# Shared expert's matmuls dealt out anew between the end of attention, the expert count, the token table and the first routed expert

## Chip, core and metric

One core of one Trainium2 chip. The metric is the device time of one launch in microseconds, lower is better. The kernel before took 885.71 us as the median of three runs (885.13 to 885.71). Its profiled execution took 885.71 us too, with a span from first to last instruction of 883.9 us.

## What is computed

Two layers in float32 on x of 16 x 128 tokens by 512. The first is cross attention with 32 query heads of 16 and 8 key heads, whose keys and values are both the context. The second is a mixture of 32 routed experts (hidden size 256) with 8 of 32 chosen per token, and one shared expert that every token passes:

```python
x = x + xattn(layernorm(x), ctx, ctx)
h = layernorm(x)
scores = sigmoid(h @ gate_weight.T)
# 4 of 8 groups by the sum of their two best, then the 8 best experts; weights * 2.5
routed = sum_e comb[:, e] * ((silu(h @ w1[e].T) * (h @ w3[e].T)) @ w2[e].T)
shared = (silu(h @ shared_w1.T) * (h @ shared_w3.T)) @ shared_w2.T
out = x + routed + shared
```

## The kernel before, in words

Line numbers are those of the kernel before. The order of instructions on PE, DVE, ACT and POOL is the order in which the program writes them (a manual schedule, line 199 on); each engine goes through its own list in order, and a matmul that waits holds back all matmuls behind it. Only waits between engines are added by the framework: for data, and for a buffer of a pool whose earlier user still reads it.

The work runs in stages:

1. *Attention* (`attention_small`), over 32 items (16 batches, two halves of the key heads): `scores`, `values`, `transposes`. While it ends, the second layernorm's rows are made (`gate_rows`), stored for the gathers, transposed into `xnT` (`turn_of`), and gate logits are taken (`gate_parts`, `gate_sums`). PSUM, eight banks of 128 x 512 float32, is shared by `ps_sc` (two tiles of two banks), `ps_x` (two banks), `ps_lg` and `ps_oT` (one each).
2. *Routing* (`route`): DVE works out the choice of experts; PE counts tokens per expert (lines 1230 and 1238), ranks them (1261 to 1280) and orders the experts (1274 to 1310).
3. *Token table*: for each of 16 token tiles, `slot_tokens` has DVE make two one-hot tiles `hr` and `hq` (line 1018), ACT scale one into `ht` (1029), and PE add eight products into `tok` (1033). `finish_tokens` (1044, 1045) turns `tok` into the table `token` that the gathers index.
4. *Routed experts*: POOL gathers token rows with indirect DMAs (1440) into eight buffers; DVE transposes them in blocks (1489); ACT and DVE copy the blocks into halves of `xall` (1486); PE multiplies. The first expert runs directly (`up`, 1521), the next 30 by a scheme of seven products (1592), for which DVE makes sums of weights (1554) and differences of tokens (1583). Expert outputs (1729) are scaled by ACT and added to the output by indirect DMAs (1701).

The *shared expert* has no stage of its own: its matmuls are fillers. `shared_up(k, i, ...)` is a generator of eight matmuls of 128x512 for token block k (of 4) and half i of the hidden size (of 2): four into a bank g (then ACT's silu, line 290), four into a bank u (then DVE's product, 293). `shared_down(b)` is two matmuls for token tile b (1370), and `add_down` adds them to x on DVE (1380) and stores x to the output. There are 64 up matmuls and 16 downs. Ups of (0,0) are drawn by `filler(n)` in attention, the other 56, in the order (0,1), (1,0), (1,1), (2,0), (2,1), (3,0), (3,1), by `up_matmuls(n)`:

| where drawn | up matmuls before |
|---|---|
| attention's end: `filler` 1, 1, 1, then 5 | 8 |
| `route`, ahead of the count (line 1138) | 20 |
| `route`, behind the ranks (1311, 1326) | 4 + 9 |
| token steps b = 0 to 6, one each (1402) | 7 |
| behind the table (1776, 1780), two calls of `2 * ND` | 8 + 8 |

Downs 0 to 7 stand at the odd token steps, downs 8 to 15 behind the last ups. There, each down is followed on DVE's list by a transpose of gathered rows, some copies, and the add of that down.

In this stretch PSUM holds `ps_y` and `ps_z` (one bank each, used in turn by the downs, and later by the routed experts' outputs), `ps_gu` (two banks for the ups), `ps_rt` (`tok` and the rank) and `ps_sm` (two small tiles). Silus and products are collected in the lists `later` and `products` and written by `evictions`, which holds a product back for one token step. Behind the last down, `ps_p` opens with six banks, in the place of `ps_gu`, `ps_rt` and `ps_sm`; the routed experts use it as a ring. The pool `late`, with the sums and the silu results of the routed experts, lies where x lay, so its first users wait for the stores of x.

Of the kernel before, what the change touches and what calls it, by code (L numbers as in the profile page):

```python
# [9 lines left out]
F32 = mybir.dt.float32  # L10
# [5 lines left out]
PSUM = bass.MemoryType.PSUM  # L16
DRAM = bass.MemoryType.DRAM

P = 128
# [27 lines left out]
def tile_xattn_moe(  # L47
# [22 lines left out]
    TB = 512  # L70
# [160 lines left out]
    def gate_rows(b, eng):  # L231
        xn = xnp.tile([P, D], F32, tag="xn2", name="xn2", bufs=4)
        normalized(xn, xs[b], b, SECOND, eng)
        nc.sync.dma_start(rows[ts(b, P), 0:D], xn)
        xn2[b] = xn
# [39 lines left out]
    def shared_up(k, i, bank, later, products):  # L275


        g, u = bank(), bank()
        sl = fp.tile([P, TB], F32, tag="ssl", name="ssl")
        for w, acc in ((0, g), (1, u)):  # L280
            for d in range(ND):
                nc.tensor.matmul(  # L282
                    acc,
                    lhsT=sup[:, w, d, ts(i, P)],
                    rhs=xnT[k][:, d, :],
                    start=(d == 0),
                    stop=(d == ND - 1),
                )
                if d == ND - 1 and w == 0:
                    later.append(lambda: nc.scalar.activation(sl, g, AF.Silu))  # L290
                if d == ND - 1 and w == 1:
                    products.append(
                        lambda: nc.vector.tensor_tensor(acts[k][:, i, :], sl, u, ALU.mult)
                    )
                yield
# [5 lines left out]
    def attention_small():  # L301


        with ExitStack() as ph:
# [134 lines left out]
            H = P // 2  # L439
            halves = [slice(h * H, (h + 1) * H) for h in range(2)]  # L440

            def transposes(*sets, pool=ps_x, between=()):


                x = pool.tile(
                    [P, 2, 2, 2, P], F32, tag=("x" if pool is ps_x else "sc"), name="x"
                )
                for s, (of, split, _) in enumerate(sets):
                    for k in range(4):
                        for h, rows in enumerate(halves):  # L450
                            if split:
                                to = x[:, h, :, s, ts(k, P // 4)]
                                by = ident[rows, rows].rearrange("p (a b) -> p a b", a=2)
                            else:
                                to = x[:, h, k // 2, s, ts(k % 2, H)]
                                by = ident[rows, rows]
                            nc.tensor.matmul(  # L457
                                to,
                                lhsT=of[rows, k, :],
                                rhs=by,  # L460
                                start=True,
                                stop=True,
                                is_transpose=True,
                                tile_position=(h * H, 0),
                            )
                for s, (_, _, then) in enumerate(sets):
                    if s == len(sets) - 1:
                        for f, a in between:
                            f(*a)
                    then(x[:, :, :, s])  # L470
# [29 lines left out]
            def values(b, i):  # L500
                oT = ps_oT.tile([P, TB], F32, tag="oT", name="oT")
                for j in range(NJ):
                    nc.tensor.matmul(  # L503
                        oT[j * HP : (j + 1) * HP],
                        lhsT=vas[b // 4 % 2][:, b % 4, 2 * j + i, :],
                        rhs=ps.pop((b, i, j)),
                        start=True,
                        stop=True,
                        tile_position=(0, j * HP),
                    )  # L510
                t = ap2.tile([P, G, P], F32, tag="oTs", name="oTs")
                nc.vector.tensor_copy(
                    t.rearrange("p g (h s) -> p h g s", h=2),
                    oT.rearrange("p (h g s) -> p h g s", h=2, g=G),
                )
                oTs[b, i] = t
# [15 lines left out]
            def added(b, i, eng=nc.gpsimd):  # L532
                return (
                    oTs.pop((b, i)),
                    True,
                    lambda x: add(b, i, x.rearrange("p h r (g e) -> p (h r) g e", e=HP), eng),
                )

            def turn_of(b, copy=nc.scalar.copy):
                def then(x):  # L540
                    copy(
                        xnT[b // 4][:, :, ts(b % 4, P)].rearrange(
                            "p (r k) (h s) -> p h r k s", r=2, h=2
                        ),
                        x.rearrange("p h r (k s) -> p h r k s", k=2),
                    )

                return xn2.pop(b).rearrange("p (k d) -> p k d", d=P), False, then
# [12 lines left out]
            def gate_parts(b):  # L561
                lgT = ps_lg.tile([P, 2 * P], F32, tag="lg", name="lgT")
                for k in range(ND):
                    nc.tensor.matmul(  # L564
                        lgT[k * E : (k + 1) * E],
                        lhsT=gw[:, k, :],
                        rhs=xnT[b // 4][:, k, ts(b % 4 // 2, 2 * P)],
                        start=True,
                        stop=True,
                        tile_position=(0, k * E),  # L570
                    )
                parts_of[b] = ap2.tile([P, 2 * P], F32, tag="lgTs", name="lgTs")
                nc.scalar.copy(parts_of[b], lgT)
# [106 lines left out]

            gate_rows(12, nc.gpsimd)
            nc.scalar.activation(table, table, AF.Sigmoid)
            values(*items[N - 1])
            transposes(added(*items[N - 2]), turn_of(11), pool=ps_sc)
            gate_rows(13, nc.gpsimd)
            gu = ps_sc.tile([P, 2, TB], F32, tag="sc", name="gu")
            banks = iter([gu[:, i] for i in range(2)])
            later, products = [], []
# [2 lines left out]
            def filler(n):  # L691
                for _ in range(n):
                    next(matmuls)

            transposes(added(*items[N - 1], nc.vector))
            gate_parts(8)
            layernorm_stats(14, SECOND)
# [6 lines left out]
            gate_sums(10, nc.scalar.copy)  # L704
            filler(1)
            transposes(turn_of(12), turn_of(13))
            gate_parts(12)
            gate_rows(15, nc.vector)
            transposes(turn_of(15), pool=ps_sc)
            gate_rows(14, nc.vector)  # L710
            transposes(turn_of(14, nc.vector.tensor_copy))
            gate_sums(12, nc.scalar.copy)
            gate_parts(14)
            gate_sums(14, nc.scalar.copy)
            filler(5)
            return later, products

    def attention_general():
# [328 lines left out]
    def experts(ups, in_order, later, products):  # L1047
# [64 lines left out]
                )  # L1112
            last[:] = [dma.ins]

        def bank():
            return ps_gu.tile([P, TB], F32, tag="gu", name="gu")

        def all_ups():
            for k, i in ups:
                yield from shared_up(k, i, bank, later, products)  # L1120

        matmuls = all_ups()
# [5 lines left out]
        def route():  # L1128
# [6 lines left out]

            sg = new([P, NT, E], "sg")
            nc.scalar.activation(sg, logits, AF.Sigmoid)
            up_matmuls(20)
            for silu in later:
                silu()  # L1140
            later.clear()
# [181 lines left out]
            nc.vector.tensor_copy(order, owner[0:1, :])  # L1323
            for k in range(NW):
                load_weights(k, True, True)
            up_matmuls(9)
            slots = new([P, NT, TOPK], "slots", home="hi")
            for b in range(NT):
                nc.vector.max(slots[:, b, :], key[:, b, :])
# [34 lines left out]

            return sr, sq, weights, flags

        def shared_down(b):
            y = (ps_y, ps_z)[b % 2].tile([P, D], F32, tag="y", name="y")
            for i in range(NI):
                nc.tensor.matmul(  # L1370
                    y,
                    lhsT=acts[b // 4][:, i, ts(b % 4, P)],
                    rhs=sdn[:, i, :],
                    start=(i == 0),
                    stop=(i == NI - 1),
                )
            products.append(lambda: add_down(b, y))
# [17 lines left out]
        for b in range(NT):  # L1395
            slot_tokens(b, sr, sq, tok, oh, evictions())
            if b == 2:
                weights()
            if b == 6:
                flags()  # L1400
            if b < 2 * ND - 1:
                up_matmuls(1)
            if b % 2:
                shared_down(next(downs))
        finish_tokens(token, tok, oh)
        early.close()
        tp = ctx.enter_context(tc.tile_pool(name="tp", bufs=2))
        pieces = []
        for k in range(E):
# [374 lines left out]
        n_copied = 3  # L1784
        downs = list(downs)
        for i, b in enumerate(downs):
            shared_down(b)
            transpose_to(min(6 + i, last_slice(3)))
            for f in copies[len(copies) * i // len(downs) : len(copies) * (i + 1) // len(downs)]:
                f()  # L1790
            for f in products:
                f()
            products.clear()
        shared.close()
        ps_p = ctx.enter_context(tc.tile_pool(name="ps_p", bufs=6, space=PSUM))
        x_only.close()
        late = ctx.enter_context(tc.tile_pool(name="late", bufs=2, side="right"))
        KEPT = 2
# [169 lines left out]
```

## Time and profile before

| what | value |
|---|---|
| profiled execution | 885.71 us |
| its span | 883.9 us |
| mean granted TensorE clock | 0.994 |
| chain that ended last, share of PE | 86% |
| of it: seven products (L1592), outputs (L1729), shared ups (L282), shared downs (L1370) | 42%, 24%, 5%, 2% |
| first to last attention matmul, about | 1 to 109 us |
| count begins / table done / first routed matmul | 141.60 / 186.53 / 219.73 us |

The profile is of one execution. A row of the timeline is: start in us, length in us, engine, line, operation, output<-inputs, shape, and in brackets the idle time of the engine ahead of it with what ended it. A float32 matmul of the program shows as two records, so 16 records of line 282 are one group's eight ups. Ends of matmuls are modelled, and a length reaches past the start of the next; starts are the better measure. Equal rows that follow each other are merged (x count). A row of waits is: who waited, for whom, total us, times, longest.

### The profile page before, as it was taken

Reading aid. Unit: us, or ns where it says so; the run is one execution under the profiler, and the core shown is the slowest. Engines: PE = TensorE matmul, PEld = TensorE weight load, DVE = VectorE, ACT = ScalarE, POOL = GpSimd, SP = SyncE. Lnnn points to the kernel's source line nnn. Section 1 sums busy time; section 2 is a strip of 40 time slices with the busy share of each in tenths; the row PEclk is TensorE's granted clock in tenths of the full one; section 3 lists DMA queues with packets and bytes.
Section 4 is the critical chain, followed back from the end, with each engine's and each line's share of the span. In section 5 each row is a group of like instructions: output and inputs, shape, how many; then the busy total and the mean of one; then the engine's idle time right before and its main releaser. Section 6 shows DMA issues by size and latency. Waiting matters only on the chain.

```text
span 883.9 us, 13625 instructions
## 1 busy us (share of the span) xinstructions
PE 864.2 (98%) x4015; PEld 540.4 (61%) x4015; DVE 626.0 (71%) x1599; ACT 689.6 (78%) x1570; POOL 479.3 (54%) x590
## 2 busy tenths in 40 slices
PE   9999989998999999999999999999999999999995
PEld 5344444543766665666666666666767777777763
DVE  7877767766887677777777777777768777777510
ACT  5888832437899898878888889898898989999831
POOL 4487550044255576656566655665555456664554
PEclk9999999999999999999999999999999999999998
DMA  9111112547367788777778777878778767776544
GB/s 303 60 48 49 49 49 86 181 150 210 109 163 163 167 195 202 165 175 185 174 172 190 182 181 187 184 191 201 196 154 196 179 165 172 197 191 163 92 76 55
DMA packets 59876, 137.15 MB, mean 155 GB/s; under 512 B 12168, under 2 KB 16392, under 8 KB 59792
## 3 DMA queue, kind: packets, MB, share of 16 engines
q0 software_dynamic: 32032, 69.25, 40.8%
q1 hardware_dynamic: 27680, 66.81, 22.3%
q8 instruction: 34, 0.56, 0.3%
q14 instruction: 50, 0.41, 0.2%
q10 hardware_dynamic: 80, 0.13, 0.0%
HBM read 96.71 MB, written 46.73 MB: 162 GB/s over the span
## 4 chain that ended last, share of the span: by engine, by line
PE 86%; issue 3%; DVE 3%; POOL 3%; DMA 2%; ACT 1%; another core or an unknown queue 0%; SPq 0%; POOLq 0%; DVEq 0%; ACTq 0%
PE p L1592 42%; PE y L1729 24%; PE gu L282 5%; PE sc L487 4%; PE oT L503 3%; POOL out_dram L1701 3%; PE y L1370 2%; PE x L457 2%; DMA out_dram<-yw,token 2%; PE gu L1521 2%; DMA cn<-in_c_dram 1%; DVE blocks L1489 1%; PE tok L1033 1%; PE lgT L564 0%; PE lg L579 0%
## 5 line engine op out<-in xcount | busy, mean ns | idle before, releaser
L1486 ACT COPY xall<-blocks 32x256 f32<-32x256 f32 (+10 forms) x1137 | 419.0, 369 | 15.1
L1701 POOL DMA_INDIRECT out_dram<-yw,token x150 | 245.1, 1634 | 211.0 <-DMA out_dram<-yw,token 73.9
L1729 PE MATMUL y<-wdn,sa 128*128 128x512 f32 (+2 forms) x672 | 259.1, 594 | 0.0
L1440 POOL DMA_INDIRECT xgs<-rows,token x138 | 154.5, 1119 | 137.1 <-DVE token L1045 57.2
L1592 PE MATMUL p<-xall,wup 128*128 128x270 f32 (+27 forms) x720 | 185.5, 394 | 0.0
L1592 PEld LDWEIGHTS p<-xall,wup 128*128 128x128 f32 x720 | 136.6, 190 | 44.3 <-issue 16.6
L1729 PEld LDWEIGHTS y<-wdn,sa 128*128 128x128 f32 (+2 forms) x672 | 100.9, 171 | 83.7 <-issue 71.7
L1745 ACT ACTIVATE yw<-y,wt 128x512 f32<-128x512 f32 x138 | 94.8, 687 | 70.7 <-PE y L1729 39.3
L1592 PE MATMUL p<-t,s 128*128 128x270 f32 (+27 forms) x480 | 125.6, 394 | 0.0
L1592 PEld LDWEIGHTS p<-t,s 128*128 128x128 f32 x480 | 91.1, 190 | 37.6 <-issue 22.4
L1489 DVE STREAM_TRANSPOSE blocks<-xgs 128x512 f32<-128x512 f32 x138 | 97.4, 706 | 0.2
L1602 DVE TENSOR_TENSOR z<-u,p 128x270 f32<-128x270 f32 (+27 forms) x96 | 48.8, 508 | 68.7 <-PE p L1592 64.5
L497 ACT ACTIVATE p<-sc 128x1024 f32<-128x1024 f32 x64 | 62.1, 1023 | 13.2 <-PE sc L487 13.2
L1592 PE MATMUL p<-t,wup 128*128 128x270 f32 (+27 forms) x240 | 63.8, 396 | 0.2 <-DVE z L1602 0.2
L1592 PE MATMUL p<-xall,s 128*128 128x270 f32 (+27 forms) x240 | 63.5, 395 | 0.4 <-DVE z L1602 0.4
L1592 PEld LDWEIGHTS p<-t,wup 128*128 128x128 f32 x240 | 44.9, 190 | 25.4 <-issue 14.8
L282 PE MATMUL gu<-xall,sup 128*128 128x512 f32 x128 | 58.1, 599 | 0.7 <-ACT ssl L290 0.7
L1602 DVE TENSOR_TENSOR u<-u,p 128x270 f32<-128x270 f32 (+27 forms) x48 | 24.4, 508 | 44.8 <-PE p L1592 36.9
L1592 PEld LDWEIGHTS p<-xall,s 128*128 128x128 f32 x240 | 45.3, 190 | 16.4 <-issue 3.7
L1486 DVE COPY xall<-blocks 32x256 f32<-32x256 f32 (+11 forms) x187 | 51.1, 297 | 3.5
L487 PE MATMUL sc<-qT,kz 32*128 32x512 f32 x256 | 44.2, 639 | 0.5 <-DVE qT L478 0.2
L1583 DVE TENSOR_TENSOR t<-xall,t 128x540 f32<-128x540 f32 (+27 forms) x60 | 43.4, 723 | 0.5
(218 smaller groups left out, 920.3 us busy)
## 6 DMA issues: line engine op xcount, KB each, us to landing
wup<-in_w_dram SPq DMA_DIRECT2D x64, 512.0 KB
wdn<-in_w_dram SPq DMA_DIRECT2D x32, 512.0 KB
rows<-xn SPq DMA_DIRECT2D x16, 256.0 KB
out_dram<-x SPq DMA_DIRECT2D x16, 256.0 KB
x<-in_x_dram SPq DMA_DIRECT2D x15, 256.0 KB
out_dram<-yw,token POOLq DMA_INDIRECT x150
xgs<-rows,token POOLq DMA_INDIRECT x138
cTs<-in_cT_dram SPq DMA_DIRECT2D x4, 256.0 KB
```

Source lines behind the costliest of these rows:

```text
L282: nc.tensor.matmul(acc, lhsT=sup[:, w, d, ts(i, P)], rhs=xnT[k][:, d, :], start=(d == 0), stop=(d == ND - 1),)
L487: nc.tensor.matmul(scs[j // 2][:, j % 2], lhsT=kzs[b // 4 % 2][rows, b % 4, i, :], rhs=qT[rows], start=True, stop=True, tile_position=(j * ...
L497: nc.scalar.activation(p, sc, AF.Exp, scale=1.0 / HD**0.5)
L1440: nc.gpsimd.indirect_dma_start(out=t, out_offset=None, in_=rows[:, :], in_offset=bass.IndirectOffsetOnAxis(ap=token[:, j : j + 1], axis=0) ...
L1486: yield on_ACT, 1 + many, lambda dst=dst, of=of, copy=copy: copy(dst, of)
L1489: nc.vector.transpose(blocks[:, j % NB_BUF, :], xgs[:, j % NG_BUF, 0:D])
L1583: yield lambda o=out_, a=a, b=b: nc.vector.tensor_tensor(o, a, b, ALU.subtract)
L1592: nc.tensor.matmul(acc[:, i, 0:h], lhsT=w[:, i, d, :], rhs=x[:, d, :], start=(first and i == d == 0), stop=(i == outs[-1] and d == 1), ski ...
L1602: soon(lambda: nc.vector.tensor_tensor(out_, a, b, ALU.add))
L1701: ins = nc.gpsimd.indirect_dma_start(out=flat, out_offset=bass.IndirectOffsetOnAxis(ap=token2[:, k - 1 : k] if a else token[0:b, j : j + 1 ...
L1729: nc.tensor.matmul(y[c0:c1, :], lhsT=acts_of[k % NA][:, i, col : col + c1 - c0], rhs=wdn[k % NW][:, i, :], start=(i == 0), stop=(i == NI - 1),
L1745: nc.scalar.activation(yws[j], y, AF.Copy, scale=wt[:, j : j + 1])
```

## The change

Five edits, all about where the shared expert's matmuls stand and which banks they use:

- In attention one `filler(1)` is put ahead of the last `values`, one behind the transposes of batches 12 and 13; the last `filler` goes from 5 to 3. The bank pair for the transposes beside them is taken ahead of the filler's pair, as before (`bank_pair` is split off from `transposes` for that).
- In `route`, 21 ups stand ahead of the count for 20, and 4 + 4 behind the ranks for 4 + 9.
- In the table, ups stand at steps 0 to 5 and at 6, 8, 10, 12, 14: 11 for 7. Behind the table it stays at 8 + 8.
- Group (1,1) uses `ps_y` and `ps_z` in place of `ps_gu`; groups (3,0) and (3,1) use the six-bank ring `ps_p`.
- `ps_p` opens right behind the table, ahead of the last 16 ups, once the open silus, products and adds are written; downs 8 to 15 use it instead of `ps_y` and `ps_z`.

```diff
             nc.scalar.activation(table, table, AF.Sigmoid)
-            values(*items[N - 1])
-            transposes(added(*items[N - 2]), turn_of(11), pool=ps_sc)
-            gate_rows(13, nc.gpsimd)
+            two = bank_pair(ps_sc)
             gu = ps_sc.tile([P, 2, TB], F32, tag="sc", name="gu")
...
+            filler(1)
+            values(*items[N - 1])
+            transposes(added(*items[N - 2]), turn_of(11), x=two)
+            gate_rows(13, nc.gpsimd)
             transposes(added(*items[N - 1], nc.vector))
...
             transposes(turn_of(12), turn_of(13))
+            filler(1)
             gate_parts(12)
...
-            filler(5)
+            filler(3)
             return later, products
...
         def all_ups():
             for k, i in ups:
+                banks = iter(
+                    [(ps_y, "y"), (ps_z, "y")]
+                    if (k, i) == (1, 1)
+                    else [(ps_p, "p")] * 2
+                    if k == NTB - 1
+                    else [(ps_gu, "gu")] * 2
+                )
...
-            up_matmuls(20)
+            up_matmuls(21)
...
-            up_matmuls(9)
+            up_matmuls(4)
...
-        def shared_down(b):
-            y = (ps_y, ps_z)[b % 2].tile([P, D], F32, tag="y", name="y")
+        def shared_down(b, pool=None):
+            y = (pool or (ps_y, ps_z)[b % 2]).tile(
+                [P, D], F32, tag="p" if pool else "y", name="y"
+            )
...
-            if b < 2 * ND - 1:
+            if b % 2 == 0 or b < 6:
                 up_matmuls(1)
             if b % 2:
                 shared_down(next(downs))
         finish_tokens(token, tok, oh)
+        for f in evictions() + evictions():
+            f()
         early.close()
+        shared.close()
+        ps_p = ctx.enter_context(tc.tile_pool(name="ps_p", bufs=6, space=PSUM))
...
         for i, b in enumerate(downs):
-            shared_down(b)
+            shared_down(b, ps_p)
...
-        shared.close()
-        ps_p = ctx.enter_context(tc.tile_pool(name="ps_p", bufs=6, space=PSUM))
         x_only.close()
```

## The prediction

> **What bounds the kernel now.** I read the page first: which engine is busy, and what share of the chain that ended last it holds.
>
> ```profile
> PE 864.2 (98%) x4015; PEld 540.4 (61%) x4015; DVE 626.0 (71%) x1599; ACT 689.6 (78%) x1570; POOL 479.3 (54%) x590
> ```
>
> TensorE is the bound: 883.9 us of span hold 19.7 us without a matmul, and PE holds 86% of the chain. So a deal of matmuls can win only idle PE time and time at a lower clock. The waits of PE say where it idles; first between 100 and 234 us, where every edit lies, then for the rest.
>
> ```profile
> PE y L1370 <- DVE x L1380: 2.8, 1, 2.8
> PE lgT L564 <- ACT xall L541: 1.2, 1, 1.2
> PE oT L503 <- DVE oTs L512: 0.9, 1, 0.9
> PE gu L282 <- ACT ssl L290: 0.7, 1, 0.7
> ...
> PE tok L1033 <- DVE x L1380: 0.5, 2, 0.3
> ```
>
> ```profile
> PE p L1592 <- DVE z L1602: 0.6, 2, 0.4
> ```
>
> Columns: total us, times, longest. Behind 234 us PE waits 0.6 us in 650, so the routed experts go at PE's pace, and what their first matmul gains should reach the end. The timeline of PE gives the stages and the unit prices.
>
> ```profile
> 119.97 21.70 PE L282 MATMUL gu<-xall,sup 128*128 128x512 f32 x50
> 141.60 0.55 PE L1230 MATMUL count<-ones,sel 128*32 128x1 f16 x16
> ```
>
> ```profile
> 157.47 0.67 PE L1033 MATMUL tok<-hq,ht 128*128 128x138 f16 x8
> 157.98 1.07 PE L282 MATMUL gu<-xall,sup 128*128 128x512 f32 x2
> 158.88 0.68 PE L1033 MATMUL tok<-hq,ht 128*128 128x138 f16 x8
> ...
> 187.46 13.90 PE L282 MATMUL gu<-xall,sup 128*128 128x512 f32 x32
> 201.19 3.60 PE L1370 MATMUL y<-sdn,sa 128*128 128x512 f32 x8
> 207.63 12.26 PE L1370 MATMUL y<-sdn,sa 128*128 128x512 f32 x24 [2.84 <-DVE x L1380]
> 219.73 13.98 PE L1521 MATMUL gu<-xall,wup 128*128 128x256 f32 x64
> ```
>
> A written up or down matmul is two records of 0.429 us (32 in 13.73 from 187.46). From start to start, one token step (8 records) takes 0.515 us, an up matmul among them 0.905, a down (two matmuls, four records) 1.72. Between these stages, the matmuls that count and rank hold PE from 141.60 to 145.19. The gap before 207.63 also costs clock: 24 records take 12.10 us where 24 x 0.429 is 10.30.
>
> ```profile
> core 0: us, PE busy (x) PEld busy (x) DVE busy (x) ACT busy (x) POOL busy (x), PEclk, DMA share, GB/s
> 200.00:205.00 5.00, 4.79 (x12) 1.81 (x10) 1.94 (x6) 4.85 (x13) 3.89 (x4) 1.00 0.70 196
> 205.00:210.00 5.00, 2.37 (x4) 1.15 (x5) 3.05 (x8) 4.86 (x12) 1.10 (x2) 0.84 0.45 145
> 210.00:215.00 5.00, 5.00 (x10) 2.00 (x9) 4.30 (x16) 4.87 (x12) 2.21 (x3) 0.82 0.84 214
> 215.00:220.00 5.00, 5.00 (x14) 2.33 (x13) 4.27 (x9) 1.69 (x5) 0.78 (x1) 1.00 0.89 273
> ```
>
> **Part by part.** All times are of the profiled execution: 885.71 us, span 883.9, and 885.71 is also the median of the runs shown.
>
> *Attention's end.* One up matmul goes in front of the last `values`, one behind the transposes of batches 12 and 13; two fewer stand at the end (3 for 5). The first falls in the 0.86 us before 106.63: PE is free at 105.77, its bank at 105.86, when the second exponential ends. The matmul ends near 106.75, so `values` may slip by 0.1; from there the tail is held at 114.28 by POOL's row 13 (done 113.75), so I charge nothing (bounds 0 and 0.86). The second falls into the 1.17 us before 116.16: transposes issued by 114.92, plus 0.86. Charge nothing; without those covers each costs 0.86.
>
> *Up to the count.* 50 records before line 1230 become 2 x (3 + 21) = 48: 21.63 us becomes 20.76, **-0.87**. PE was late here: DVE's `sel` ended at 140.22, the count began at 141.60; it will begin near 140.73. The 21st matmul would need the bank of a product that DVE makes only behind the count; group (1,1) therefore sits in `ps_y` and `ps_z`, which nobody uses until the first down. DVE's routing behind the count moves with it.
>
> *Count to table.* The 13 matmuls between 145.19 and 157.47 (12.28 us: 11.16 of records, the rest the 0.75 wait for a `gu` bank) become 8: 6.87 us, **-5.41**. The wait goes: the bank wanted is now that of (1,0), freed at DVE's product near 143.7 before, 0.9 sooner then. Step 0 of the table needs ACT's `ht`, which began at 150.61 and takes 1.15; 0.87 sooner it ends at 150.9, and PE comes at 151.2.
>
> *Table.* 16 token steps, 11 ups (7 before) and 8 downs: 8.24 + 9.95 + 13.76 = 31.95 us for 29.99, **+1.96**. The old stretch held 28.34 of such work and 1.65 of waits; with four ups put at steps 8 to 14, a pair of steps costs PE 2 x 0.515 + 0.905 + 1.72 = 3.66, DVE 2 x (0.60 + 0.64) + 0.61 = 3.09, ACT 2 x 1.1. So I let those waits vanish (bound: +1.65 if all stay). PE ends here at 183.15 for 187.46; `tok` is complete near 181.6, the table near 182.2 for 186.53, and POOL's first gather starts 4.2 us sooner.
>
> *Behind the table.* 16 up matmuls, 13.73 both times. They now open the six-bank ring, in banks that `tok`, the rank, the counts and `gu` held. DVE reads `tok` out by 182.2 and does the product of (2,1) by 182.9; PE comes at 183.15: no charge, and 0.75 if it must also await the add of down 7, which DVE can start only then. Each gather still has some 8 us before its transpose, because DVE's transposes stay behind the product of (3,0) (8.4 us before, 8.1 after). Then eight downs: 18.54 us become 32 x 0.429 = 13.74, **-4.80**, being 3.00 of gap and 1.80 of clock. In `ps_y` and `ps_z` down 10 needed the add of down 8, which DVE began only at 206.88:
>
> ```profile
> 206.88 0.69 DVE L1380 TENSOR_TENSOR x<-y,x 128x512 f32<-128x512 f32 x1 [3.46 <-remote]
> ```
>
> In the ring, downs 8 and 9 take banks 5 and 6, 10 to 13 those of the ups, and the first to need that add is down 14, some 207.2. DVE's 3.46 us has no releaser in the trace. If it comes again at that instruction, the add ends near 203, so 4 us of cover remain.
>
> A rule speaks against the 1.80. The Trainium skill, "TensorE: Matmul & The Clock Gate", Part 1, has the clock halve after an idle window of some 3.4 us, and its windows run free, so a 2.84 us gap need not cost clock at all. By the rule closing it gives 3.0 and the sum below is 7.3; by the row the clock sank to 0.84 and 0.82, and it is 9.1. I take the row.
>
> *What is late next.* The add of down 15 ended at 220.62; its store released the `late` buffers at 222.78, where DVE's weight sums start. With DVE's gap again, adds run from 202.35 for 12.6 us, and the release comes near 217.1, 5.7 sooner, while PE is 9.1 sooner. Token sum t2 was ready at 231.42 and used at 234.73: 3.3 of cover against 3.4 of loss. I charge 0.2. Without the gap nothing is charged. ACT's copies for pieces 0 and 1 follow the silu of (3,1) and move 4.3, but the first 12 (0.43 each) end near 199 and PE wants them at 210.6.
>
> **Sum.** -0.87 - 5.41 + 1.96 - 4.80 = -9.1, plus 0.2: 885.71 - 8.9 = **876.8 us**. Cross-check: waits and clock removed 1.12 + 1.65 + 3.00 + 1.80 = 7.57, two matmuls into idle 1.72, and 0.18 for four ups at 0.905 instead of 0.86.
>
> **Rivals.**
> *A new wait takes the old one's place* (14%). DVE's unexplained gap comes twice as long: t2 is 0.2 + 3.5 = 3.7 us late, PE idles for it and pays 1.8 of clock again: 876.6 + 5.5 = 882.1. Shorter gaps fill 878 to 882. For it: the gap has no cause in view and lies among gathers (DMA share 0.70). Against: DVE idles like that once in the execution.
> *Table steps keep their waits, and the swap of banks awaits down 7* (12%): 876.8 + 1.65 + 0.75 = 879.2. For it: DVE and ACT already stop PE at two steps. Against: 3.66 over 3.09 per pair.
> *It doesn't reach the end* (4%): a DMA or POOL pace behind 234 us would leave about 885.5. For it: DMA is busy 0.74 there. Against: PE's 0.6 us of waits.
> *Slower* (3%): the ring now chains the first expert's banks to adds 10 to 15, which stand behind DVE's transposes and so behind gathers. Add 10 is due by 205.7 and PE wants its bank at 210.6. Only lateness of more than 4.9 + 9.1 = 14 us turns the sum; at 16 it gives 887.7. Fourteen gathers drained in 20.5 us (186.84 to about 207.4); they would have to take 36.
>
> **Chances.** The forecast has 67%, with 875.6 to 878.0 as its own range. The range for 8 in 10 runs from 875.6, where bounds on the good side end (noise of 0.6 between runs, and the extra 0.2), to 880.8, through the second rival and the lower part of the first. Below 883.9 (over 0.2% faster, about what a measurement can tell from no change): 0.93; within 0.2%: 0.04; slower: 0.03.
>
> **What will show it.** Right: the count at about 140.7; first token step at 151.2; the table near 182.2; no PE gap between 183 and 224 and a granted clock of 1.00 there; first routed matmul at 210.6; PE's waits behind that still under 1 us. Wrong: PE waits at the first matmul behind the table, at token steps 8 to 15, or on `t` and `s` at expert 1; or PE's first expert 9 us sooner with the end unmoved.

## The result and the profile after

The changed kernel took **881.59 us** as the median of six runs (881.41 to 882.98), the kernel before 885.76 beside it (also six, 885.13 to 888.69): a ratio of 0.9951, 95% interval 0.9937 to 0.9965. It is faster, by 4.2 us and not by the 8.9 forecast; 881.59 lies above the range. Its profiled execution took 881.58 us with a span of 879.7, to be set against 885.71 and 883.9.

The page of after, busy time and share of the engines:

```profile
PE 861.7 (98%) x4015; PEld 538.5 (61%) x4015; DVE 625.9 (71%) x1599; ACT 689.4 (78%) x1570; POOL 476.4 (54%) x590
```

The idle part of the span is 18.0 us for 19.7: TensorE lost nearly as much as before, so idle time must have moved. The waits of PE of after, first from 100 to 224 us, then from 224 to 880 (total us, times, longest):

```profile
PE lgT L566 <- ACT logits L584: 0.6, 2, 0.3
PE lg L581 <- ACT lgTs L575: 0.5, 1, 0.5
PE x L459 <- DVE oTs L514: 0.3, 1, 0.3
```

```profile
PE p L1612 <- ACT p L1661: 2.0, 1, 2.0
PE p L1612 <- DVE z L1622: 1.1, 2, 0.7
PE p L1612 <- DVE t L1603: 1.1, 1, 1.1
```

All waits that the prediction wanted to remove are gone from the first table. In the second, the prediction's 0.6 us have become 4.2. The timeline of PE of after (line numbers of the changed kernel stand up to 20 above those of before):

```profile
120.18 20.85 PE L282 MATMUL gu<-xall,sup 128*128 128x512 f32 x48
140.96 0.55 PE L1244 MATMUL count<-ones,sel 128*32 128x1 f16 x16
...
151.52 0.67 PE L1038 MATMUL tok<-hq,ht 128*128 128x138 f16 x8
...
183.65 13.90 PE L282 MATMUL gu<-xall,sup 128*128 128x512 f32 x32
197.38 13.90 PE L1386 MATMUL y<-sdn,sa 128*128 128x512 f32 x32
211.11 13.98 PE L1541 MATMUL gu<-xall,wup 128*128 128x256 f32 x64
224.93 1.35 PE L1612 MATMUL p<-xall,wup 128*128 128x352 f32 x4
227.36 2.63 PE L1612 MATMUL p<-t,s 128*128 128x352 f32 x8 [1.09 <-DVE t L1603]
...
234.86 1.45 PE L1612 MATMUL p<-xall,wup 128*128 128x352 f32 x4 [1.97 <-ACT p L1661]
...
238.63 1.45 PE L1612 MATMUL p<-t,wup 128*128 128x352 f32 x4 [0.73 <-DVE z L1622]
```

Up to 211.11 the stages fall where the prediction put them, within 0.6 us, and the downs run as one block. Then TensorE waits three times in fourteen microseconds, 3.79 us together. The stretches of 5 us that showed the lost clock before, now of after:

```profile
core 0: us, PE busy (x) PEld busy (x) DVE busy (x) ACT busy (x) POOL busy (x), PEclk, DMA share, GB/s
205.00:210.00 5.00, 5.00 (x13) 2.26 (x12) 4.88 (x14) 4.88 (x11) 2.86 (x3) 1.00 0.69 157
210.00:215.00 5.00, 5.00 (x22) 3.82 (x22) 4.77 (x14) 2.88 (x8) 0.99 (x1) 1.00 0.95 316
```

The granted clock is 1.00 for 0.84 and 0.82. VectorE's gap ahead of the add of down 8 did come again (timeline of DVE of after, the row that answers to 206.88):

```profile
203.16 0.69 DVE L1396 TENSOR_TENSOR x<-y,x 128x512 f32<-128x512 f32 x1 [3.57 <-PE y L1386]
```

What holds TensorE at expert 1 is told by the chain that ended last (start, length, what), of after:

```profile
197.54 5.60 PE y L1386 x12
203.16 0.69 DVE x L1396
...
214.97 0.70 DVE x L1396
215.69 2.85 DMA out_dram<-x
218.65 0.38 ACT sg L1551
...
234.36 0.46 ACT p L1661
...
238.14 0.45 DVE z L1622
238.63 6.18 PE p L1612 x20
```

Behind the table the chain leaves TensorE. It goes through VectorE's adds, the store of the last tile of x, and the silu that this store lets start (`sg` lies in the pool `late`, where x lay). From there it is ScalarE's list, silus and copies without a pause up to the copy of p (in the texts below "copy p"), 218.65 to 234.36: 15.71 us. Then 4.27 us over VectorE's `z` to the next matmul that waits for it; this matmul reads `t` and `wup`, so what it waits for is a bank that `z` reads. The same rows of before, ACT's timeline, then PE's, and between them TensorE's products up to the copy, from the chain of before:

```profile
222.76 0.38 ACT L1531 ACTIVATE sg<-gu 128x256 f32<-128x256 f32 x1 [6.02 <-DMA out_dram<-x]
...
235.70 2.75 ACT L1486 COPY xall<-blocks 32x96 f32<-32x96 f32 x7
238.48 0.45 ACT L1641 COPY p<-p 128x352 f32<-128x352 f32 x1
```

```profile
233.71 4.75 PE p L1592 x16
```

```profile
242.75 1.45 PE L1592 MATMUL p<-t,wup 128*128 128x352 f32 x4 [0.22 <-DVE z L1602]
```

15.72 us from silu to copy, and 4.27 to z: the same list, begun 4.11 us later than after the change. And TensorE already waited 0.22 us for its end. The list ended 4.12 us sooner (238.63 for 242.75), and so did the program (4.13).

### The profile page after: what moved, and what is told of

Read it like the earlier page. It is cut to its first block, busy times and chain, and to the rows that moved or that the text cites. A ratio compares the mean times of both kernels' runs of the same rounds, so it can differ in the third digit from the quotient of the medians.

```text
span 879.7 us, 13628 instructions
## 1 busy us (share of the span) xinstructions
PE 861.7 (98%) x4015; PEld 538.5 (61%) x4015; DVE 625.9 (71%) x1599; ACT 689.4 (78%) x1570; POOL 476.4 (54%) x590
## 4 chain that ended last, share of the span: by engine, by line
PE 88%; POOL 3%; ACT 3%; issue 2%; DVE 2%; DMA 2%; POOLq 0%; ACTq 0%
PE p L1612 42%; PE y L1749 24%; PE gu L282 6%; PE sc L489 5%; PE oT L505 4%; PE x L459 2%; PE y L1386 2%; POOL out_dram L1721 2%; ACT xall L1506 2%; DMA out_dram<-yw,token 1%; PE tok L1038 1%; DVE x L1396 1%; PE lgT L566 0%; PE lg L581 0%; DVE xall L1506 0%
## 5 line engine op out<-in xcount | busy, mean ns | idle before, releaser
L1460 POOL DMA_INDIRECT xgs<-rows,token x138 | 150.7, 1092 | 134.5 <-DVE token L1050 53.2
L1612 PE MATMUL p<-xall,wup 128*128 128x270 f32 (+27 forms) x720 | 185.6, 394 | 2.0 <-ACT p L1661 2.0
L1612 PEld LDWEIGHTS p<-xall,wup 128*128 128x128 f32 x720 | 136.5, 190 | 46.6 <-issue 16.1
L1612 PE MATMUL p<-t,s 128*128 128x270 f32 (+27 forms) x480 | 125.7, 394 | 1.1 <-DVE t L1603 1.1
L1612 PEld LDWEIGHTS p<-t,s 128*128 128x128 f32 x480 | 91.0, 190 | 39.0 <-issue 22.4
L1612 PE MATMUL p<-t,wup 128*128 128x270 f32 (+27 forms) x240 | 63.8, 396 | 0.7 <-DVE z L1622 0.7
L1612 PE MATMUL p<-xall,s 128*128 128x270 f32 (+27 forms) x240 | 63.6, 396 | 0.5 <-DVE z L1622 0.4
L1612 PEld LDWEIGHTS p<-t,wup 128*128 128x128 f32 x240 | 45.0, 190 | 25.9 <-issue 14.1
L1612 PEld LDWEIGHTS p<-xall,s 128*128 128x128 f32 x240 | 45.2, 190 | 16.9 <-issue 4.3
```

What stands on the lines that cost most here:

```text
L1460: nc.gpsimd.indirect_dma_start(out=t, out_offset=None, in_=rows[:, :], in_offset=bass.IndirectOffsetOnAxis(ap=token[:, j : j + 1], axis=0) ...
L1612: nc.tensor.matmul(acc[:, i, 0:h], lhsT=w[:, i, d, :], rhs=x[:, d, :], start=(first and i == d == 0), stop=(i == outs[-1] and d == 1), ski ...
```

## The experiments

**The theories.** L, the late release: the end follows the last add of x, its store, and the 15.7 us of ScalarE behind it; what TensorE gains ahead of that is lost at expert 1. P, TensorE's own account: the end follows TensorE's list, so the ring's 4.8 us count by themselves. R, the ring: the six banks, tied to the adds, hold expert 1 back. The first four kernels ran on one chip (kernel before there: 884.49, 19 runs), each an edit of the changed kernel. Their expected times count from 885.7 and 881.6, so on this chip they are all some 1.2 us too high. The changed kernel itself did not run there; it is set beside them by its ratio, 0.9951, and by its profile.

*banks_only*: the new banks with the old deal.

```diff
-            filler(1)
             values(*items[N - 1])
...
-            filler(1)
             gate_parts(12)
...
-            filler(3)
+            filler(5)
...
-            up_matmuls(21)
+            up_matmuls(20)
...
-            up_matmuls(4)
+            up_matmuls(9)
...
-            if b % 2 == 0 or b < 6:
+            if b < 2 * ND - 1:
```

> The new banks with the old deal: fillers 1, 1, 1, 5 in attention, 20 ups ahead of the count, 4 + 9 behind the ranks, 7 in the table; (1,1) in ps_y and ps_z, (3,0), (3,1) and downs 8 to 15 in the ring of six. Theory L (the end is set by the last add of x, its store, the release of the pool late, and then ACT's list of 15.7 us up to the copy p of expert 1, which in the changed kernel began only 4.1 us sooner than before): the ring takes away PE's gap of 3.0 and 1.8 of clock, but DVE's adds lose only the 1.1 us in which they waited for PE, so the time is near 884.6. Rival P (PE's account holds, and what was lost is the deal's part): 885.7 - 4.8 = 880.9, or 0.75 less if the wait for a gu bank goes too.

Measured: 884.44 us, ratio 0.9998 (0.9987 to 1.0009). No gap of PE among the downs, and nothing gained. PE's timeline of banks_only:

```profile
201.85 13.90 PE L1384 MATMUL y<-sdn,sa 128*128 128x512 f32 x32
215.58 13.98 PE L1539 MATMUL gu<-xall,wup 128*128 128x256 f32 x64
...
237.78 1.45 PE L1610 MATMUL p<-xall,wup 128*128 128x352 f32 x4 [1.78 <-ACT p L1659]
```

The first routed matmul came 4.15 us sooner than in before's profile, the release only 1.20 (221.56 for 222.76), and the profiled end 1.20. P, at 880.9 or, from this chip's 884.49, at 879.7, falls. L says 883.4 from 884.49; that lies just inside the interval (883.3 to 885.3), but the 1.1 us that it promised do not show in the medians.

*deal_only*: the new deal, with downs 8 to 15 in their two old banks.

```diff
-            shared_down(b, ps_p)
+            shared_down(b)
```

> The changed kernel with downs 8 to 15 back in ps_y and ps_z (the ring stays for the ups (3,0) and (3,1)). Theory L: PE gets its gap of 3 us and the slow clock back and reaches the first routed matmul near 215.9, but the last add of x moves by no more than 1.1 us, so 882.4 (881.6 to 882.8). Rival P: 881.6 + 4.8 = 886.4. Rival R (the ring itself holds expert 1, since its banks are chained to the adds): faster than the changed kernel, 880 or less.

Measured: 880.13 us, ratio 0.9954 (0.9936 to 0.9972), as much as the whole change. PE's timeline and ACT's of deal_only:

```profile
197.25 5.52 PE L1386 MATMUL y<-sdn,sa 128*128 128x512 f32 x12
205.05 9.34 PE L1386 MATMUL y<-sdn,sa 128*128 128x512 f32 x20 [2.28 <-DVE x L1396]
214.23 13.98 PE L1541 MATMUL gu<-xall,wup 128*128 128x256 f32 x64
```

```profile
217.49 0.38 ACT L1551 ACTIVATE sg<-gu 128x256 f32<-128x256 f32 x1 [4.70 <-DMA out_dram<-x]
...
233.21 0.45 ACT L1661 COPY p<-p 128x352 f32<-128x352 f32 x1
```

PE's gap is back and its first routed matmul is 3.12 us behind that of after, yet copy p is 1.15 ahead of it and so is the end (880.41 for 881.58, in the two profiled executions). P falls here too. L's own number was 2.3 us too high. Some 1.2 of it is the chip; for the rest, VectorE's gap came one add later in this execution and was shorter (2.50 us, ahead of the add of down 9), so the release was already at 217.49. The time is near R's 880 as well, but R asked for less than the changed kernel takes, and by the ratios (0.9954 and 0.9951) it is the same. The next two keep the ring and decide between L and R.

*no_stores*: the tiles 8 to 15 of x + shared are not stored, so this half of the output lacks them.

```diff
-            nc.sync.dma_start(out[b], xs[b])
+            if b < 8:
+                nc.sync.dma_start(out[b], xs[b])
```

> The changed kernel without the stores of x for token tiles 8 to 15, so that half of the output lacks x and the shared part; everything else is as it was. Theory L: late is released by the last add (215.66) and not by its store (218.65), ACT's and DVE's first work in it starts 3.0 us sooner, and the time is 881.6 - 3.0 = 878.6. Rival R (banks): no change, 881.6.

Measured: 877.85 us, ratio 0.9921 (0.9906 to 0.9937), near L's number and not R's. DVE's timeline of no_stores, then ACT's: the weight sums and the silu now start right behind the last add, not when a store lands.

```profile
214.38 0.69 DVE L1396 TENSOR_TENSOR x<-y,x 128x512 f32<-128x512 f32 x1
215.10 0.69 DVE L1575 TENSOR_TENSOR s<-wup 128x512 f32<-128x512 f32 x1
```

```profile
215.30 0.39 ACT L1552 ACTIVATE sg<-gu 128x256 f32<-128x256 f32 x1 [2.08 <-PE gu L1542]
```

The last add ended at 215.07. The row names TensorE, but TensorE's part was done earlier: in *early_sg* below, where this silu waits for no store, it starts 1.92 us behind the first routed matmul, which would be 213.34 here. Of the 3.35 us that the silu gained on after (218.65), 0.59 come from a shorter gap of VectorE (2.65 us for 3.57, the last add ends at 215.07 for 215.66) and the rest from the missing store.

*sg_apart*: the silu results in a pool of their own, not where x lay; all else as in the changed kernel.

```diff
-                sl = late.tile([P, 2, M], F32, tag="sg", name="sg", bufs=3)
+                sl = sgs.tile([P, 2, M], F32, tag="sg", name="sg", bufs=3)
...
-                t = late.tile([P, 4 * M if name == "z" else TB], F32, tag=name, name=name, bufs=bufs)
+                t = (sgs if name == "sg" else late).tile([P, 4 * M if name == "z" else TB], F32, tag=name, name=name, bufs=bufs)
...
+        sgs = ctx.enter_context(tc.tile_pool(name="sgs", bufs=3))
         x_only.close()
```

> The changed kernel with the silu results of the routed experts (tile sg, three buffers) in a pool of their own that does not lie where x lay; the sums stay in late. Theory L: ACT's first silu no longer waits for the stores and its list ends some 5 us sooner, so PE's wait of 1.97 for the copy p goes; DVE's weight sums still start at 218.67, so the waits of 1.09 for t and 0.73 for z stay: 879.6. Rival R: 881.6.

Measured: 878.60 us, ratio 0.9935 (0.9919 to 0.9951). The waits for p and t are gone, 0.7 us for z are left. Both runs keep the ring and its banks: L stands, R falls. ScalarE's list started at 213.04 but took 17.95 us, since it now waits for transposes that stand on VectorE's list behind the weight sums, which still lie in `late`. ACT's timeline of sg_apart:

```profile
213.04 0.38 ACT L1551 ACTIVATE sg<-gu 128x256 f32<-128x256 f32 x1
...
222.10 2.06 ACT L1506 COPY xall<-blocks 32x256 f32<-32x256 f32 x5 [2.25 <-DVE blocks L1509]
```

The pool's own share is small, as an estimate: VectorE's gap was 1.93 us here, so `late` was free at 216.38. Had `sg` waited for that too, copy p would stand 15.7 us later, near 232.1; it stands at 230.99, 1.1 sooner.

The law behind these runs, from the profiled executions. "Behind z" is the matmul of L1612 (or its shifted line) that waits for VectorE's `z`, the row of 238.63 above:

| kernel | first routed matmul | first silu `sg` | copy p | behind z | profiled time | time less behind z |
|---|---|---|---|---|---|---|
| before | 219.73 | 222.76 | 238.48 | 242.75 | 885.71 | 642.96 |
| after | 211.11 | 218.65 | 234.36 | 238.63 | 881.58 | 642.95 |
| banks_only | 215.58 | 221.56 | 237.28 | 241.55 | 884.51 | 642.96 |
| deal_only | 214.23 | 217.49 | 233.21 | 237.49 | 880.41 | 642.92 |
| no_stores | 211.42 | 215.30 | 231.03 | 235.30 | 878.24 | 642.94 |
| sg_apart | 211.11 | 213.04 | 230.99 | 235.25 | 878.22 | 642.97 |

The last column is the same to 0.05 us, so nothing behind this matmul differs; the time of the first routed matmul explains nothing. In each of these the matmul stands 4.26 to 4.28 us behind copy p, and TensorE waits for it. From silu to copy p it is 15.71 to 15.73 us in all but *sg_apart*.

**VectorE's gap, and a faster version.** On the next chip (before: 881.67, 11 runs) I asked what the gap ahead of the add of down 8 is: F, a pause at a fixed place of VectorE's list, or G, a wait that belongs to the gathers in flight. With these ran *early_sg*, which tests what L says can be gained.

*shift6*, *shift40*: 6 or 40 short writes more on VectorE, behind the add of down 7 (n is 6 or 40). They took 0.7 and 5.0 us of the 6.25 us in which VectorE stood idle there, so they delayed nothing themselves.

```diff
+        spare = oh.tile([P, 1], F32, tag="spare", name="spare")
+        for _ in range(n):
+            nc.vector.memset(spare, 0.0)
```

> The changed kernel with six one-element memsets on DVE behind the add of down 7, where DVE is idle, so that all later DVE instructions stand six places further on. Theory F (DVE's gap of 2 to 3.6 us is a wait for DVE's own code, at a fixed place in its list): the gap moves some six instructions ahead, to about the fifth transpose, ahead of the product of (3,1). Theory G (the gap is a wait for something that the gathers in flight hold up, tied to the work): it stays between that product and the first adds, 2 to 3.6 us long.

> The same with forty memsets, some 2.5 us of DVE's idle 6 us there. Theory F: the place of the gap comes to lie among the table's steps, where no gather is in flight, and the gap of 3.5 us goes; adds, store and release of late come sooner by it: 878.1 to 879 by the changed kernel's 881.6. Theory G: no change in time or gap.

*hold*: `gather_next` in `transpose_to` only from the sixth transpose on.

```diff
-                gather_next()
+                if n_turned > 5:
+                    gather_next()
```

> The changed kernel with gathers 8 to 13 held back: none is issued for the first five transposes, so POOL's list has eight gathers in flight, which drain before the first add, and issues the others from the sixth transpose on. Theory G, and F as well if the code's transfer stands behind gathers: the gap goes, the release of late comes up to 3.5 us sooner, 878.1 to 879. If the gap has nothing to do with gathers: it stays, 881.6. Should later gathers come too late instead, DVE waits at the ninth or tenth transpose, and the time is 881.6 or more.

Measured: 878.85 (one run), 877.24 and 877.41 us, ratios of the last two 0.9946 (0.9925 to 0.9968) and 0.9941 (0.9921 to 0.9961). None of the three had a gap, so they told nothing of its cause. And *hold* turned out to be no edit: it moves the place in the program where gathers are written, but every engine's list kept its order, so it is the changed kernel run again.

*early_sg*: *sg_apart*, and downs 8 to 11 with their transposes, copies and adds stand ahead of the ups of (3,1), so that VectorE's train of adds starts earlier.

```diff
-        up_matmuls(2 * ND)
-        for f in evictions() + evictions():
-            f()
...
         for i, b in enumerate(downs):
+            if i == 4:
+                up_matmuls(2 * ND)
+                for f in evictions() + evictions():
+                    f()
             shared_down(b, ps_p)
```

> The changed kernel with sg in a pool of its own, and downs 8 to 11 with their adds, transposes and copies put between the ups of (3,0) and those of (3,1), where DVE idles. Theory L: four adds and stores come in DVE's idle 2.4 us, the last add some 2 us sooner, and with ACT free of the stores no wait of PE is left at expert 1: 881.6 - 4.5 = 877.1, and 877.9 if the 0.7 us wait for z stays. Rival P2 (behind the table all of PE's gain is now in, and the end is held elsewhere): as sg_apart, 878.6.

Measured: **876.29 us** (876.12 to 876.42), ratio 0.9929 (0.9913 to 0.9944); the changed kernel, as *hold*, had 877.41 (877.24 to 877.56) beside it, so *early_sg* gains 1.1 us on it. Its expected 877.1 was near by luck: it took 4.5 us off the 881.6 of a chip with VectorE's gap. On this chip the gap was missing, and TensorE lost little at expert 1 to begin with (0.64 us of wait for z in hold). What *early_sg* is worth where the gap comes was not run. The chain of early_sg:

```profile
204.28 7.12 PE y L1386 x16
211.41 13.81 PE gu L1541 x64
225.22 4.73 PE p L1612 x16
229.96 1.72 PE y L1749 x4
231.67 8.28 PE p L1612 x28
```

It is TensorE alone, with no wait behind 120 us: here the forecast's picture holds. It is the fastest of the kernels that ran on this chip.

**Is the gap the chip's?** Theory C says that the gap comes on some chips and not on others. On a third chip (before: 881.48, 17 runs) kernels ran again, the first two unedited.

> The kernel before as it is, with a profile on the chip of the three runs beside it. On the chip of the last group it took 881.7 us where it took 885.7 and 884.5 on the two before. Theory C (DVE's gap ahead of the first adds comes on some chips and not on others): 881.7 with no gap in DVE and no wait of PE for the add, or 884.5 to 886 with a gap of 2 to 3.6 us. If the gap is the same on all chips: the gap whatever the time.

> The changed kernel as it is, beside the one before on one chip. By theory L the difference is the shift of the release of late: 4.1 where both have the gap or neither has, since then the adds move with the table: with a gap 881.6, without one 877.5 to 878.

> The changed kernel with forty memsets on DVE in its idle time, beside the changed kernel on one chip. Theory F (gap is DVE's code at a fixed place of its list): no gap, and 3 us under the changed kernel if that has the gap. Theory G (gap tied to gathers): the gap stays. Theory C with a chip without the gap: the same as the changed kernel, to 0.3 us.

> The changed kernel with gathers 8 to 13 held back to the sixth transpose, beside the changed kernel on one chip. Theory G: no gap, and 3 us under the changed kernel if that has the gap. Theory F with the code's transfer not hindered by gathers: the gap stays. On a chip without the gap: the same as the changed kernel, to 0.5 us.

Measured: *before_again* 882.37 (ratio 1.0006, 0.9995 to 1.0018), *after_again* 877.47 (0.9957, 0.9940 to 0.9973), *shift40_again* 877.53 (0.9962, 0.9948 to 0.9976), *hold_again* 877.55 (0.9960, 0.9946 to 0.9974). No gap in any of them, kernel before included. DVE's first add behind the table in after_again:

```profile
199.62 0.69 DVE L1396 TENSOR_TENSOR x<-y,x 128x512 f32<-128x512 f32 x1
```

So the gap goes with the chip, or with what was true of it at the time, and with it both kernels are some 4 us slower: 885.8 and 881.6, against 881.5 and 877.5. For the changed kernel the profiles account for it: the first add stands 3.54 us later with the gap (203.16 for 199.62) and the store took 0.85 longer, which makes the silu 4.39 later (218.65 for 214.26) and the end 4.44. The profiled execution of before_again, 884.67, was its slowest for another reason, told in the last section: it lost clock ahead of the count, which came 3.2 us later than in before.

The change is worth the same 4 us either way. With the gap it is the release that gives them. Without it the two accounts come out alike. In after_again the chain still runs over store, `sg` (214.26), copy p (229.98, again 15.72) and z (234.25), with 642.89 to the end, but TensorE waits only 0.36 us for that z, and 0.57 in before_again (there copy p stands at 237.46 with 647.21 left, as in before, where 885.71 less 238.48 is 647.23). From the count to the first routed matmul TensorE needs 73.56 us in before_again and 70.16 in after_again, 3.40 less; from the count to the silu it is 76.94 and 73.32, 3.62 less. To both come the 0.85 us that the count gains on what stands ahead of it, measured between before and after. So there the forecast's account is right once the 4.8 us of the ring are left out, since there is no gap to close: 9.1 less 4.8 is 4.3.

A fourth chip had the gap again (before 885.01, one run each), so F and G were asked anew.

> The changed kernel as it is, a control: does VectorE's gap ahead of the first adds come on this chip? With it some 4 us longer than without it: first store release near 218.6 and a wait of TensorE for p of about 2 us at the first routed experts, as against 214.3 and none.

> Six short VectorE writes of a spare column more, behind the add of down 7. If the control has the gap: by the theory of a fixed place in VectorE's list it comes six instructions earlier, ahead of a transpose or copy instead of an add; by the theory of the gathers it stays where they drain, near the add of down 8, with the same end to within 0.5 us.

> Forty such writes, some 2.5 us of VectorE's time, at the same place. If the control has the gap: by the theory of a fixed place it goes from the first adds altogether and stands some forty instructions earlier, within or ahead of the writes; by the theory of the gathers it stays with the add of down 8 and is shorter only by what the writes take.

> The gathers that are issued while the first transposes are written are held back. If the control has the gap: by the theory of the gathers the gap goes or is under 1 us; by the theory of a fixed place it stays at 2 to 3.6 us at the same instruction.

Measured: 880.72, 881.15, 880.91 and 880.88 us. The rows of DVE around the gap, of after_gap and then of shift40_gap:

```profile
197.63 0.69 DVE L293 TENSOR_TENSOR sa<-ssl,gu 128x512 f32<-128x512 f32 x1 [2.33 <-issue]
...
203.13 0.69 DVE L1396 TENSOR_TENSOR x<-y,x 128x512 f32<-128x512 f32 x1 [3.54 <-PE y L1386]
```

```profile
201.11 0.69 DVE L293 TENSOR_TENSOR sa<-ssl,gu 128x512 f32<-128x512 f32 x1 [5.83 <-PE y L1386]
...
203.08 0.69 DVE L1396 TENSOR_TENSOR x<-y,x 128x512 f32<-128x512 f32 x1
```

Six writes left it where it was (3.65 us, same add). Forty put it ahead of the product of (3,1), six instructions earlier, and the same length (201.11 for 197.63 is 3.48 more). A pause at a fixed place would have moved by six and by forty: F falls in this form. *hold*, being no edit, cannot speak for or against G (3.64 us, same add). The cause stays open.

## Why the prediction was wrong, step by step

*Attention's end, 0:* measured +0.21. `values` began at 106.83 for 106.63, the last ups at 120.18 for 119.97; the 0.1 of slip was 0.2.

*Up to the count, -0.87:* right; 120.18 to 140.96 is 20.78 for 21.63, -0.85.

*Count to table, -5.41:* right; 140.96 to 151.52 is 10.56 for 15.87, -5.31. The wait for a bank went.

*Table, +1.96:* +2.14; 151.52 to 183.65 is 32.13 for 29.99. The waits of before vanished as assumed, the rival that kept them was wrong. The table was done at 182.72, 0.5 later than said. TensorE did not wait for the add of down 7 either.

*Behind the table, -4.80:* right on TensorE: 16 ups and 8 downs took 13.73 us each, and the first routed matmul stood at 211.11, 8.62 sooner for the 9.1 forecast. The clock's 1.80 came back too, as the row said. But *banks_only* shows what this term is worth at the end: nothing, and *deal_only* that giving it up costs nothing. The prediction's cross-check closes with this only if its last 0.18 is taken off: 7.57 + 1.72 - 0.18 = 9.11.

*What is late next, +0.2:* **this step failed; it measured 4.49 us** (8.62 at the first routed matmul, 4.13 at the end). Two of its terms were wrong.

- The cover. The prediction took 3.3 us, read at token sum t2, which was used at 234.73. There it was right: 4.5 us lost less 3.3 is 1.2, and TensorE waited 1.09 us for `t`. But the same release also starts ScalarE's list, and that had none: of ScalarE it checked only the copies for the first two pieces. In before the seven copies ahead of copy p ended at 235.70 + 2.75 = 238.45, and TensorE's product that it copies ended at 238.46: a tie. From there the matmul behind z is 4.27 us away, and TensorE, with its own work between, still waited 0.22. So on this path the cover was 0, not 3.3 us.
- The release. Forecast 217.1, measured 218.65, so 4.11 sooner and not 5.7. VectorE's train of adds began 3.72 sooner (203.16 for 206.88; forecast 202.35) and took 12.5 us as forecast (13.74 before), which gives 4.96. But the last store needed 2.99 us from the last add's end to the silu, for 2.14 in before: 0.85 given back.

The sum closes: TensorE 8.62 sooner, the release 4.11 sooner, cover nil, leaves 4.51 lost; measured 4.49.

The evidence was in the prediction's own table: the 0.6 us of waits for z behind 234 us, of which 0.22 is this one (the other 0.38 comes at 272.86). It was read as "only 0.6 us, so TensorE sets the pace". But where a wait shows at all, however short, no cover is left.

*The rivals.* The first, a new wait in place of the old, gave 882.1 and came near the time, but not by its mechanism: VectorE's gap was 3.57 us for 3.46 before and not doubled, and the clock stayed at 1.00. Of the signs named as wrong, a wait on `t` came (1.1 us); the larger one, for p, was not on the list. The second rival did not come. The third, that the gain does not reach the end, was half right (4.49 of 8.62 us stayed behind), but the pace was that of ScalarE behind the release, not of DMA or POOL. That the ring ties expert 1 to the adds cost nothing measurable: *sg_apart* keeps the ring and has no wait for p or `t`, and no profile shows TensorE waiting for an add at expert 1.

## What to carry to other kernels

A buffer that a later stage inherits makes the earlier stage's last store the start of that stage; follow each engine that starts with that release to its first consumer, not one of them. Where the engine that sets the pace shows even a short wait, take the cover there as zero, and credit it only with what moves the chain behind the wait. Before counting a gap that was closed, ask whether the chain behind it starts from the gap's other side: here VectorE's gap stayed, and only TensorE stopped waiting for it.

## What the runs showed of the hardware

- VectorE's gap of 1.9 to 3.7 us behind the table came in all ten profiles taken where the kernel before needed 884.5 to 885.8 us, and in none of the eight taken where it needed 881.5 to 881.7. In all ten the instruction behind it is one that reads what TensorE wrote. Neither cause proposed for it was shown.
- The two gaps of TensorE differ in clock. In before, 2.84 us and then a granted clock of 0.84 and 0.82, with 1.80 us lost over 24 records; in finer stretches it is 0.50 from 208.5 to 211 us, 0.60 to 212 and 1.00 behind. In *deal_only*, 2.28 us and a granted clock of 1.00 throughout; its 20 records took 0.60 us more than 8.58 (205.05 to 214.23), which is then not clock. The Trainium skill's idle window of some 3.4 us (TensorE: Matmul & The Clock Gate, Part 1) is longer than both. That a halved clock can follow a gap shorter than the window is shown; what decides is not. Length alone does not: in before_again TensorE waited 1.17, 0.32 and 0.53 us between 115 and 120 us, the clock was 0.50 from 119 to 125, and the count came at 144.80 for 141.60 in before; before has waits of 1.17, 0.32 and 0.54 us there and kept 1.00.
- The last store of x, 256 KB, took 2.0 to 2.9 us to land in the chains of after_again, deal_only and after (2.00, 2.23, 2.85).
